# Softmax attention over 128 heads of eight features: a sixth exponential per group on the vector engine, squares on GpSimd, and keys, queries and squares loaded in another order

## The chip, the cores and the metric

The kernel runs on one core of one Trainium2 chip. The engines are called as the profile calls them: PE (TensorE, matmuls), PEld (its weight loads), ACT (ScalarE), DVE (VectorE), POOL (GpSimd) and SP (SyncE, which here only issues DMAs). The metric is the device time of one execution in microseconds (us); lower is better. A median over several executions is given, and one further execution was taken with the hardware profiler.

## The reference, cut to what matters

Four graph layers work on a matrix of 3327 nodes by 128 features, each as `x = x + layer(relu(layernorm(x)), adj)`. The first of them is the one this document is about:

```python
def _L0_gnn_ref(x, spatial_encoding, edge_encoding, Wq, Wk, Wv, Wo):
    n, d = x.shape                      # 3327, 128
    h = Wq.shape[0] // d                # 8
    scale = d ** (-0.5)
    q = (x @ Wq.T).reshape(d, n, h)
    k = (x @ Wk.T).reshape(d, n, h)
    v = (x @ Wv.T).reshape(d, n, h)
    a = jnp.einsum('dnh,dmh->dnm', q, k) * scale
    a = a + spatial_encoding + edge_encoding       # both are adj
    a = jax.nn.softmax(a, axis=2)
    out = jnp.einsum('dnm,dmh->dnh', a, v)
    return out.reshape(n, h * d) @ Wo.T
```

So there are d = 128 independent heads, each with a 3327 x 3327 score matrix of inner length 8, to which twice the adjacency matrix is added before the softmax. The other three layers are two hyperbolic graph layers and a degree-normalised message layer; they multiply the adjacency matrix with a 3327 x 128 matrix and are not touched.

## The kernel before, in words

The program has three stretches. In the first (to about 420 us of the profiled span) the queries, keys and values of all heads are made and written to HBM. The second, the attention, runs from about 420 to 10170 us. The third does the other layers.

**Tiling of the attention.** The scores are made transposed: keys lie on the 128 partitions, queries on the free axis. The 3327 queries are cut into seven chunks `c` of `CW` = 476 columns (the last has 472). The 128 heads form 32 groups `g` of four heads `j`. The 26 tiles of 128 keys form 13 pairs `q` of two tiles (`r` = 0 and 1). The loops run over `c`, then `g`, then `q`; one pair is called `u`, and there are 7 x 32 x 13 = 2912 of them in 224 groups.

**What is done for one pair.** Each of the two key tiles has one PSUM bank of the seven banks of `S`. `seed` (L645, DVE) writes the bank with adjacency minus a bound (`a - shb`, both tiles in SBUF). `scores` (L654, PE) adds the first head's products; `exps` (L666, ACT) reads both banks at once, 952 columns, and writes the exponentials `e`. For head `j` + 1 the matmul adds that head's products and takes away those of head `j` in the same pass: the stacked queries `QS` hold the head's rows and the negated rows of the head before. So a pair's four exponentials follow one another in the same two banks. Where the two banks are not neighbours (one pair in seven) ACT does two instructions of 476 columns instead (L669). `values` (L713, PE) multiplies `e` with the values `VA` and accumulates in one further bank, `po`, over the 13 pairs of a group; after that `store` copies it out on DVE (L721) and sends it off with four DMAs from POOL's queue (L725).

**Exponentials by hand.** In the pairs `q` of `BY_HAND` = (0, 2, 5, 7, 10), the exponential of head 0 on tile r = 1 is not done by ACT but by DVE, with a polynomial (`hand_exp`). There the bank is not seeded for head 0. DVE reads the bare scores out of the bank into the tile `h` (L691), then seeds the bank, then does three scalar_tensor_tensor steps (L695) and a last one (L697) that multiplies by the exponential of adjacency minus bound (`EA`, made once per chunk by `shifted`, L678, and `bare`, L683). Head 1 then uses `QZ`, queries without the negated rows. ACT does one instruction of 476 columns for that slot instead of one of 952.

**The order is written out by hand.** The loop `for i in range(-4, 4 * n + 15)` issues one slot `i` at a time under `tc.manual_schedule()`: the order in which instructions are issued here is the order on each engine. Slot `i` holds the exponential of head `j = -i % 4` of pair `u = (i - 3j) / 4`, so ACT alternates between four pairs. On odd slots PE gets the scores of the next two slots and then eight value matmuls (four heads of one tile; each is two instructions in the profile). DVE gets, in the order of slots that belong to a pair u by hand: at 4u the copy L691 and `seed(u, 1)`, at 4u+1 `seed(u+1, 1)`, at 4u+2 `seed(u+2, 0)`, at 4u+3 the first polynomial step, at 4u+4 two more, at 4u+7 the last. `heads_of` makes the value matmul that needs the hand-made exponential come one pair late.

**Loads.** `loads(u)` is called in the slot 4u and loads the next group: `load_k` (L551, 16 DMAs of 16 partitions), `load_q` (L562 and L564: six small DMAs for a head, nine for head 1), `load_v` (L575). `negate_q` (L570) copies head j's queries negated into the rows of head j + 1, after which `load_q` of head j + 1 overwrites half the rows; so these follow one another: load 0, negate 0, load 1, negate 1, load 2, negate 2, load 3. `spread_v` (L580) and `all_here` (L584, a tiny copy that waits for all key loads) are on POOL. All loads are issued from SP's queue, in the order of the program. For the next chunk, `load_adj` (L590) loads 26 adjacency tiles during the last group, and 22 times in the attention a `Square` of the adjacency matrix is transposed for later use: `load` (L283, with a small memset on POOL, L284), `turn` (L288, DVE), `largest` (L292, DVE) and `store` of 1.66 MB. `plan` puts these in slots.

Of the kernel before, what the change touches and what calls it, by code (L numbers as in the profile page):

```python
# [10 lines left out]
F32 = mybir.dt.float32  # L11
# [6 lines left out]
ALU = mybir.AluOpType  # L18
# [4 lines left out]
P = 128  # L23
N = 3327
D = 128
H = 8
HD = D * H
NT = 26
NP = NT * P
NQ = NT // 2  # L30

KW = NP // 4
HEADS = D
# [3 lines left out]
CW = 476  # L37
# [8 lines left out]
NOTHING = -1.0e30  # L46


EXP_C = (0.9999990463256836, 2.2162604331970215, 2.4563632011413574, 1.8291265964508057)
EXP_ARG = 0.9023826718330383  # L50
BY_HAND = (0, 2, 5, 7, 10)
LN_EPS = 1e-5
L1_EPS = 1e-7
L1_MAX_TANH = 1.0 - 1e-6
# [34 lines left out]
def gnn_kernel(ctx: ExitStack, tc: tile.TileContext, x, adj, Wq, Wk, Wv, Wo, embed, layer,  # L89
               embed_bias, layer_bias, weight, bias, W_in, W_out, out):  # L90
    nc = tc.nc
# [14 lines left out]
    kS_d = dram.tile([2, H, HEADS, NP], F32, name="kS_d")  # L106
# [418 lines left out]
    with tc.tile_pool(name="e1", bufs=1) as e1, tc.tile_pool(name="e_adj", bufs=28) as e_adj, \  # L525
# [12 lines left out]
        S = e_ps.tile([P, 7, 512], F32, name="S")  # L538
        po = e_ps.tile([P, 512], F32, name="po")

        def load_k(c, g):

            b = (c * NG + g) % 2
            for j in range(4):
                d = 4 * g + j
                k0, nk = max(0, j - 1), 1 if j in (0, 3) else 2
                for r in range(2):
                    r0 = 64 * r + 32 * (1 - j % 2)
                    k_d = kS_d[:, :, d, r * NQ * P:(r + 1) * NQ * P].rearrange("i e n -> (i e) n")
                    for i in range(2):  # L550
                        nc.sync.dma_start(KT[b][r0 + 16 * i:r0 + 16 * i + 16, k0:k0 + nk, :].bitcast(F32),  # L551
                                          k_d.unsqueeze(1).to_broadcast([16, nk, NQ * P]))

        def load_q(c, g, j):

# [11 lines left out]
        def negate_q(c, g, j):  # L567

            b, w = (c * NG + g) % 2, width_of(c)
            nc.gpsimd.tensor_scalar(QS[b][:, j + 1, :w], QS[b][:, j, :w].bitcast(F32),  # L570
                                    -1.0, 0.0, op0=ALU.mult, op1=ALU.add)

        def load_v(c, g):
            v = e2.tile([P, 4, NT * H], F32, name="VR", bufs=1)
# [24 lines left out]
        with tc.If(loose < 1), tc.manual_schedule():  # L599
# [39 lines left out]
            def bank(u, r):  # L639
                return S[:, banks(u)[r], :width_of(pairs[u][0])]  # L640
# [19 lines left out]

            def exps(u, j):
                w, (even, odd) = width_of(pairs[u][0]), banks(u)
                e = e_of[u, j] = e_e.tile([P, 2, CW], F32, name=f"e{j}", bufs=(5, 4, 3, 2)[j])
                hand = j == 0 and by_hand(u)
                if even > odd and not hand:
                    touch(u, (0, 1), nc.scalar.activation(e[:, :, :w], S[:, odd:even + 1, :w], AF.Exp, scale=2.0))  # L666
                    return
                for r in range(1 if hand else 2):
                    touch(u, [r], nc.scalar.activation(e[:, 1 - r, :w], bank(u, r), AF.Exp, scale=2.0))  # L669

            def by_hand(u):

                return 0 <= u < n and pairs[u][2] in BY_HAND

            def shifted(c, q):

                w = width_of(c)
                nc.vector.tensor_tensor(EA[q][:, :w], adj_of[c][2 * q + 1][:, :w], shift_of[c][:, :w], op=ALU.subtract)  # L678

            def bare(c, q):  # L680

# [3 lines left out]
            def hand_exp(u):  # L685


                w = width_of(pairs[u][0])
                s = e_h.tile([P, CW], F32, name="h")[:, :w]
                e = e_of[u, 0][:, 0, :w]  # L690
                touch(u, [1], nc.vector.tensor_scalar(s, bank(u, 1), EXP_ARG, None, op0=ALU.mult))  # L691
                seed(u, 1)
                yield
                for k in (3, 2, 1):
                    nc.vector.scalar_tensor_tensor(e, s if k == 3 else e, EXP_C[k], s, op0=ALU.add, op1=ALU.mult)  # L695
                    yield
                nc.vector.scalar_tensor_tensor(e, e, EXP_C[0], EA[pairs[u][2]][:, :w], op0=ALU.add, op1=ALU.mult)  # L697

            def heads_of(u, r):


                first = (u, r)
                if by_hand(u) and r == 1:
                    first = (u + 1, 0)
                elif by_hand(u - 1):
                    first = (u, 1) if r == 0 else (u - 1, 1)
                return [first] + [(u, r)] * 3

            def values(u, r):
                c, g, q = pairs[u]  # L710
                w, k = width_of(c), c * NG + g
                for j, (v, of) in enumerate(heads_of(u, r)):
                    nc.tensor.matmul(po[32 * j:32 * j + H + 1, :w], VA[k % 2][:, 2 * pairs[v][2] + of, j, :],  # L713
                                     e_of[v, j][:, 1 - of, :w], start=(q == 0 and r == 0),
                                     stop=(q == NQ - 1 and r == 1))

            def store(u):
# [9 lines left out]
            def loads(u):  # L727

                c, g, q = pairs[u]
                k = c * NG + g  # L730
                if k + 1 < NC * NG:
                    nxt = divmod(k + 1, NG)
                    if q == 1:
                        load_k(*nxt)
                        load_q(*nxt, 0)
                        v_of[k + 1] = load_v(*nxt)
                    if q in (3, 5, 7):
                        negate_q(*nxt, q // 2 - 1)
                        load_q(*nxt, q // 2)
                    if q == 8:  # L740
                        spread_v(*nxt, v_of.pop(k + 1))
                        here[k + 1] = all_here(*nxt)
                if c + 1 < NC and (g, q) == (0, 0):
                    plan_squares(c)
                if g == NG - 1 and c + 1 < NC:
                    if q == 0:
                        shift_of[c + 1] = load_shift(c + 1)
                        adj_of[c + 1] = []
                    while len(adj_of[c + 1]) < min(NT, 2 * q + 6):
                        adj_of[c + 1].append(load_adj(c + 1, len(adj_of[c + 1])))  # L750


# [2 lines left out]
            def plan(u, f, *a):  # L755
                behind.setdefault(u, []).append((f, a))

            def plan_squares(c):
                for k, s in enumerate(range(squares_of(c), squares_of(c + 1))):
                    sq, u = Square(e_t, s), (c * NG + 7 * k + 1) * NQ  # L760
                    for j in range(4):
                        plan(u, sq.load, j)
                        plan(u + 4, sq.turn, j, 0)
                        plan(u + 9, sq.turn, j, 1)
                        plan(u + 12, sq.largest, j)
                        u += NQ
                    for k, f in ((0, sq.gather), (1, sq.back), (7, sq.finish), (8, sq.store)):
                        plan(u + k, f)

            v0 = load_v(0, 0)  # L770
            load_k(0, 0)
            load_q(0, 0, 0)
            shift_of[0] = load_shift(0)
            for j in range(3):
                negate_q(0, 0, j)
                load_q(0, 0, j + 1)
            spread_v(0, 0, v0)
            here[0] = all_here(0, 0)
            adj_of[0] = [load_adj(0, t) for t in range(NT)]

            for c in range(NC):
                for q in BY_HAND:
# [724 lines left out]
```

## Time and profile before

| what | value |
|---|---|
| median of 3 executions | 10982.34 us (10980.81 to 10985.29) |
| the profiled execution's own time | 10981.96 us |
| its span in the profile | 10980.2 us |
| granted TensorE clock, mean | 0.985 |
| busy: PE, ACT, DVE, POOL | 10533.5, 10033.1, 8487.1, 1529.1 us |
| first and last exponential of the attention (start) | 462.5 and 10167.6 us |
| DMA | 1256.98 MB, mean 114 GB/s |

The attention takes 88 per cent of the span, 9705 us for 224 groups, 43.3 us each. Busy time is the time in which at least one instruction of the engine is open; ACT's and PE's instructions overlap with their followers, so a busy share near 100% does not yet say that the engine could not go faster. In the timeline a row gives the start in us, the length in us, the engine, the line, what is written from what, how many instructions of a kind followed one another, and in brackets the idle time before the row and what ended it.

### The profile page before, as it was taken

To read this page: it belongs to the slowest core of one execution; us is meant where nothing else is said; L and a number is where in the kernel's file an instruction comes from. 1 tells how busy PE (TensorE), PEld (TensorE's weight loads), DVE (VectorE), ACT (ScalarE), POOL (GpSimd) and SP (SyncE) were. 2 spreads that over 40 slices of the span, in tenths; PEclk is the share of its full clock that TensorE was granted. 3 is DMA by queue.
4 is the path that set the end of the run, shared out by engine and by line. 5 is a ranking of instruction groups with operands and counts; after the bars stand their busy time and mean duration, and the time that the engine had idled before them with its cause. 6 is when DMAs were issued, how large, how long until landed. Compare 5 with 4: busy or idle time off the path is not lost. (4 is left out here: it accounts for less than half of the span.)

```text
span 10980.2 us, 204474 instructions
## 1 busy us (share of the span) xinstructions
PE 10533.5 (96%) x72876; PEld 3435.7 (31%) x72876; DVE 8487.1 (77%) x13503; ACT 10033.1 (91%) x13789; POOL 1529.1 (14%) x2477
## 2 busy tenths in 40 slices
PE   4599999999999999999999999999999999999889
PEld 2133333333333333333333333333323333333544
DVE  5588887888878887788887888878877777777655
ACT  3599999999999999999999999999999999999330
POOL 5011111111111111111111111111111111111101
PEclk7799999999999999999999999999999999999999
DMA  8766566565566565565556565565556555554668
GB/s 250 250 99 97 94 96 113 93 98 96 89 118 97 93 97 88 106 98 97 90 95 119 94 96 93 95 119 95 87 93 98 96 95 86 82 88 71 206 233 281
DMA packets 695339, 1256.98 MB, mean 114 GB/s; under 512 B 195218, under 2 KB 555049, under 8 KB 691244
## 3 DMA queue, kind: packets, MB, share of 16 engines
q1 hardware_dynamic: 644044, 1114.42, 55.7%
q0 software_dynamic: 50272, 129.37, 4.3%
q8 instruction: 587, 9.62, 0.4%
q14 instruction: 436, 3.57, 0.2%
HBM read 1096.53 MB, written 146.60 MB: 113 GB/s over the span
## 5 line engine op out<-in xcount | busy, mean ns | idle before, releaser
L666 ACT ACTIVATE e<-S 128x952 f32<-128x952 f32 (+1 forms) x9024 | 8357.9, 1099 | 36.7 <-PE S L654 29.4
L713 PE MATMUL po<-e,VA 128*9 128x476 f32 (+1 forms) x46592 | 5737.5, 564 | 33.0 <-DVE OS L721 12.3
L645 DVE TENSOR_TENSOR S<-a,shb 128x476 f32<-128x476 f32 (+1 forms) x5824 | 3937.9, 676 | 1447.6 <-ACT e L666 1059.4
L654 PE MATMUL S<-QS,KT 64*128 64x476 f32 (+1 forms) x22176 | 4528.6, 445 | 79.7 <-DMA a<-adjT 28.4
L654 PEld LDWEIGHTS S<-QS,KT 64*128 64x128 f32 x22176 | 2073.7, 184 | 5100.5 <-issue 1301.3
L669 ACT ACTIVATE e<-S 128x476 f32<-128x476 f32 (+1 forms) x4128 | 2467.5, 711 | 1.1 <-PE S L654 0.6
L695 DVE SCALAR_TENSOR_TENSOR e<-e,h 128x476 f32<-128x476 f32 (+1 forms) x2240 | 1497.8, 669 | 77.0
L713 PEld LDWEIGHTS po<-e,VA 128*9 128x9 f32 x46592 | 691.0, 88 | 1606.6 <-issue 1488.1
L570 POOL TENSOR_SCALAR QS<-QS 128x476 fp32r<-128x476 f32 (+1 forms) x672 | 485.6, 723 | 4312.1 <-DMA QS<-qS_d 2612.2
L725 POOL DMA_DIRECT2D oT_d<-OS x896 | 470.5, 530 | 3668.8 <-DVE OS L721 3625.5
L691 DVE TENSOR_SCALAR h<-S 128x476 f32<-128x476 f32 (+1 forms) x1120 | 728.0, 650 | 300.9 <-PE S L654 296.5
L697 DVE SCALAR_TENSOR_TENSOR e<-e,EA 128x476 f32<-128x476 f32 (+1 forms) x1120 | 759.6, 678 | 0.0
L695 DVE SCALAR_TENSOR_TENSOR e<-h 128x476 f32<-128x476 f32 (+1 forms) x1120 | 743.1, 663 | 0.0
L1107 PE MATMUL pu<-strip,y 128*128 128x512 f32 (+2 forms) x1456 | 600.5, 566 | 31.7 <-DVE y L968 14.8
L654 PE MATMUL S<-QZ,KT 64*128 64x476 f32 (+1 forms) x1120 | 493.4, 441 | 11.9 <-DVE S L645 10.5
L1107 PEld LDWEIGHTS pu<-strip,y 128*128 128x128 f32 (+1 forms) x1456 | 271.9, 191 | 305.8 <-issue 272.1
L1111 DVE TENSOR_REDUCE deg<-strip 128x1 f32<-128x1536 f32 (+1 forms) x104 | 193.8, 1881 | 63.7 <-DMA strip<-adjT 44.1
L580 POOL COPY VA<-VR 128x832 f32<-128x832 f32 x224 | 242.3, 1082 | 0.0
L654 PEld LDWEIGHTS S<-QZ,KT 64*128 64x128 f32 x1120 | 205.1, 183 | 92.2 <-DVE S L645 52.4
L288 DVE STREAM_TRANSPOSE cols<-rows 128x416 f32<-128x416 f32 x208 | 204.5, 988 | 30.3 <-DMA rows<-in_adj_dram 22.6
L1060 ACT COPY uT<-pu 128x512 f32<-128x512 f32 (+1 forms) x21 | 11.1, 555 | 222.6 <-PE pu L1107 222.6
L721 DVE COPY OS<-po 128x476 f32<-128x476 f32 (+1 forms) x224 | 146.3, 653 | 87.3 <-PE po L713 87.3
(255 smaller groups left out, 1958.6 us busy)
## 6 DMA issues: line engine op xcount, KB each, us to landing
KT<-kS_d SPq DMA_DIRECT2D x1792, 208.0 KB
KT<-kS_d SPq DMA_DIRECT2D x1792, 104.0 KB
VR<-v_d SPq DMA_DIRECT2D x224, 416.0 KB
QS<-qS_d SPq DMA_DIRECT2D x3072, 14.9 KB
QS<-qS_d SPq DMA_DIRECT2D x1536, 29.8 KB
adjT<-cols SPq DMA_DIRECT2D x26, 1664.0 KB
a<-adjT SPq DMA_DIRECT2D x156, 238.0 KB
strip<-adjT POOLq DMA_DIRECT2D x39, 895.5 KB, 5.1
```

What stands on the lines that cost most here:

```text
L570: nc.gpsimd.tensor_scalar(QS[b][:, j + 1, :w], QS[b][:, j, :w].bitcast(F32), -1.0, 0.0, op0=ALU.mult, op1=ALU.add)
L580: nc.gpsimd.tensor_copy(VA[(c * NG + g) % 2][:, :, :, 0:H], v.rearrange("p j (t e) -> p t j e", e=H))
L645: touch(u, [r], nc.vector.tensor_tensor(bank(u, r), adj_of[c][2 * q + r][:, :w], shift_of[c][:, :w], op=ALU.subtract))
L654: x = nc.tensor.matmul(bank(u, r), KT[b][64 * r:64 * r + 64, max(0, j - 1), q * P:(q + 1) * P], q_s[64 * r:64 * r + 64, :w], start=hand an ...
L666: touch(u, (0, 1), nc.scalar.activation(e[:, :, :w], S[:, odd:even + 1, :w], AF.Exp, scale=2.0))
L669: touch(u, [r], nc.scalar.activation(e[:, 1 - r, :w], bank(u, r), AF.Exp, scale=2.0))
L691: touch(u, [1], nc.vector.tensor_scalar(s, bank(u, 1), EXP_ARG, None, op0=ALU.mult))
L695: nc.vector.scalar_tensor_tensor(e, s if k == 3 else e, EXP_C[k], s, op0=ALU.add, op1=ALU.mult)
L697: nc.vector.scalar_tensor_tensor(e, e, EXP_C[0], EA[pairs[u][2]][:, :w], op0=ALU.add, op1=ALU.mult)
L713: nc.tensor.matmul(po[32 * j:32 * j + H + 1, :w], VA[k % 2][:, 2 * pairs[v][2] + of, j, :], e_of[v, j][:, 1 - of, :w], start=(q == 0 and r ...
L725: nc.gpsimd.dma_start(oT_d[:, d * N + c * CW:d * N + c * CW + w], o[32 * j:32 * j + H + 1, :w])
L1107: nc.tensor.matmul(ps[:, :k], y[:m, t, :], s[:m, c * 4 * P - c0:c * 4 * P - c0 + k], start=(t == 0), stop=(t == NT - 1))
```

## The change

* A sixth pair is done by hand: `BY_HAND` becomes (0, 2, 4, 6, 8, 10).
* The polynomial has another form. DVE copies out the scores plus a constant (`z`), POOL squares `z` (a `tensor_tensor` on GpSimd), and DVE does three scalar_tensor_tensor steps. DVE does four instructions per hand exponential where it did five, and POOL one.
* None of DVE's later steps is issued in the slot 4u+3 any more: two are issued at 4u+4 and the last at 4u+7, as far as the next pair is not by hand. `heads_of` is gone; the value matmuls are all in their normal place, and `e0` has four buffers where it had five.
* `negate_q` goes from POOL to DVE. The queries of heads 1, 2 and 3 are loaded in pairs 6, 8 and 10 (3, 5 and 7 before), each right after the negation of the head before. The queries of head 0 are issued ahead of the keys.
* The keys are loaded by 12 DMAs of 32 partitions. The values are loaded in pair 3 (1 before), and `spread_v` and `all_here` go to pair 12 (8 before).
* A square is loaded in pair 3 (0 before), turned in pairs 10 and 12 (4 and 9 before), and stored in pair 2 of the group after (8 before). Adjacency tiles for the next chunk are loaded two tiles later.
* The loads of the very first group are reordered: all queries, the shift and four adjacency tiles, the keys, the values, the other adjacency tiles; its negations are six POOL instructions on 32 partitions each.

```diff
-BY_HAND = (0, 2, 5, 7, 10)
+Q_AT = (1, 6, 8, 10)
+BY_HAND = (0, 2, 4, 6, 8, 10)
...
-        def load_k(c, g):
+        def load_k(c, g, j):
...
+                for k in range(k0, k0 + nk):
+                    nc.sync.dma_start(KT[b][r0:r0 + 32, k, :].bitcast(F32), bass.AP(
...
-            nc.gpsimd.tensor_scalar(QS[b][:, j + 1, :w], QS[b][:, j, :w].bitcast(F32),
-                                    -1.0, 0.0, op0=ALU.mult, op1=ALU.add)
+            nc.vector.tensor_scalar(QS[b][:, j + 1, :w], QS[b][:, j, :w].bitcast(F32), -1.0, None, op0=ALU.mult)
...
-                e = e_of[u, j] = e_e.tile([P, 2, CW], F32, name=f"e{j}", bufs=(5, 4, 3, 2)[j])
+                e = e_of[u, j] = e_e.tile([P, 2, CW], F32, name=f"e{j}", bufs=(4, 4, 3, 2)[j])
...
-                touch(u, [1], nc.vector.tensor_scalar(s, bank(u, 1), EXP_ARG, None, op0=ALU.mult))
+                touch(u, [1], nc.vector.tensor_scalar(z, bank(u, 1), EXP_C[0], None, op0=add))
+                nc.gpsimd.tensor_tensor(e, z, z, op=mult)
                 seed(u, 1)
                 yield
-                for k in (3, 2, 1):
-                    nc.vector.scalar_tensor_tensor(e, s if k == 3 else e, EXP_C[k], s, op0=ALU.add, op1=ALU.mult)
-                    yield
-                nc.vector.scalar_tensor_tensor(e, e, EXP_C[0], EA[pairs[u][2]][:, :w], op0=ALU.add, op1=ALU.mult)
-
-            def heads_of(u, r):
...
+                v(z, e, EXP_C[1], z, op0=add, op1=add)
+                yield
+                v(e, e, EXP_C[2], z, op0=add, op1=mult)
+                yield
+                v(e, e, EXP_C[3], EA[pairs[u][2]][:, :w], op0=add, op1=mult)
...
+                    if q in Q_AT:
+                        j = Q_AT.index(q)
+                        if j:
+                            negate_q(*nxt, j - 1)
+                        load_q(*nxt, j)
                     if q == 1:
-                        load_k(*nxt)
-                        load_q(*nxt, 0)
+                        for j in range(4):
+                            load_k(*nxt, j)
+                    if q == 3:
                         v_of[k + 1] = load_v(*nxt)
-                    if q in (3, 5, 7):
-                        negate_q(*nxt, q // 2 - 1)
-                        load_q(*nxt, q // 2)
-                    if q == 8:
+                    if q == 12:
                         spread_v(*nxt, v_of.pop(k + 1))
                         here[k + 1] = all_here(*nxt)
...
-                        plan(u, sq.load, j)
-                        plan(u + 4, sq.turn, j, 0)
-                        plan(u + 9, sq.turn, j, 1)
+                        plan(u + 3, sq.load, j)
+                        plan(u + 10, sq.turn, j, 0)
+                        plan(u + 12, sq.turn, j, 1)
...
-                    for k, f in ((0, sq.gather), (1, sq.back), (7, sq.finish), (8, sq.store)):
+                    for k, f in ((0, sq.gather), (1, sq.back), (2, sq.store), (7, sq.finish)):
...
+            for j in range(4):
+                load_q(0, 0, j)
+            shift_of[0] = load_shift(0)
+            adj_of[0] = [load_adj(0, t) for t in range(4)]
+            for j in range(4):
+                load_k(0, 0, j)
             v0 = load_v(0, 0)
...
-                for k in range(0 if at % 3 else 1 if at else 0 if by_hand(i // 4) else 2):
+                for k in range(0 if at % 3 or by_hand(i // 4) else 1 if at else 2):
```

More of the change, by code (lines that the diff above doesn't have):

```diff
@@ L46 @@
 NOTHING = -1.0e30
-EXP_C = (0.9999990463256836, 2.2162604331970215, 2.4563632011413574, 1.8291265964508057)
-EXP_ARG = 0.9023826718330383
-BY_HAND = (0, 2, 5, 7, 10)
+EXP_C = (0.25674915313720703, 0.05050157010555267, 1.8002841472625732, 0.8117094039916992)
+EXP_LEAD = -0.2054332047700882
+Q_AT = (1, 6, 8, 10)
+BY_HAND = (0, 2, 4, 6, 8, 10)
 LN_EPS = 1e-5
@@ L539, in gnn_kernel @@
         po = e_ps.tile([P, 512], F32, name="po")
-        def load_k(c, g):
+        def load_k(c, g, j):
             b = (c * NG + g) % 2
[L544 to L552, printed above, removed]
+            d = 4 * g + j
+            k0, nk = max(0, j - 1), 1 if j in (0, 3) else 2
+            for r in range(2):
+                r0 = 64 * r + 32 * (1 - j % 2)
+                for k in range(k0, k0 + nk):
+                    nc.sync.dma_start(KT[b][r0:r0 + 32, k, :].bitcast(F32), bass.AP(
+                        tensor=kS_d.tensor, offset=kS_d.offset + d * NP + r * NQ * P,
+                        ap=[[0, 2], [H * HEADS * NP, 2], [HEADS * NP, 8], [1, NQ * P]]))
         def load_q(c, g, j):
@@ L677, in shifted @@
                 w = width_of(c)
-                nc.vector.tensor_tensor(EA[q][:, :w], adj_of[c][2 * q + 1][:, :w], shift_of[c][:, :w], op=ALU.subtract)
+                nc.vector.scalar_tensor_tensor(EA[q][:, :w], adj_of[c][2 * q + 1][:, :w], EXP_LEAD, shift_of[c][:, :w],
+                                               op0=ALU.add, op1=ALU.subtract)
             def bare(c, q):
@@ L688, in hand_exp @@
                 w = width_of(pairs[u][0])
-                s = e_h.tile([P, CW], F32, name="h")[:, :w]
+                v, add, mult = nc.vector.scalar_tensor_tensor, ALU.add, ALU.mult
+                z = e_h.tile([P, CW], F32, name="h")[:, :w]
                 e = e_of[u, 0][:, 0, :w]
-                touch(u, [1], nc.vector.tensor_scalar(s, bank(u, 1), EXP_ARG, None, op0=ALU.mult))
+                touch(u, [1], nc.vector.tensor_scalar(z, bank(u, 1), EXP_C[0], None, op0=add))
+                nc.gpsimd.tensor_tensor(e, z, z, op=mult)
                 seed(u, 1)
                 yield
-                for k in (3, 2, 1):
-                    nc.vector.scalar_tensor_tensor(e, s if k == 3 else e, EXP_C[k], s, op0=ALU.add, op1=ALU.mult)
-                    yield
-                nc.vector.scalar_tensor_tensor(e, e, EXP_C[0], EA[pairs[u][2]][:, :w], op0=ALU.add, op1=ALU.mult)
-            def heads_of(u, r):
[L702 to L707, printed above, removed]
+                v(z, e, EXP_C[1], z, op0=add, op1=add)
[3 more added lines that the diff above has]
+                v(e, e, EXP_C[3], EA[pairs[u][2]][:, :w], op0=add, op1=mult)
             def values(u, r):
@@ L711, in values @@
                 w, k = width_of(c), c * NG + g
-                for j, (v, of) in enumerate(heads_of(u, r)):
-                    nc.tensor.matmul(po[32 * j:32 * j + H + 1, :w], VA[k % 2][:, 2 * pairs[v][2] + of, j, :],
-                                     e_of[v, j][:, 1 - of, :w], start=(q == 0 and r == 0),
+                for j in range(4):
+                    nc.tensor.matmul(po[32 * j:32 * j + H + 1, :w], VA[k % 2][:, 2 * q + r, j, :],
+                                     e_of[u, j][:, 1 - r, :w], start=(q == 0 and r == 0),
                                      stop=(q == NQ - 1 and r == 1))
@@ L748, in loads @@
                         adj_of[c + 1] = []
-                    while len(adj_of[c + 1]) < min(NT, 2 * q + 6):
+                    while len(adj_of[c + 1]) < min(NT, 2 * q + 4):
                         adj_of[c + 1].append(load_adj(c + 1, len(adj_of[c + 1])))
@@ L761, in plan_squares @@
                     for j in range(4):
-                        plan(u, sq.load, j)
-                        plan(u + 4, sq.turn, j, 0)
-                        plan(u + 9, sq.turn, j, 1)
+                        plan(u + 3, sq.load, j)
+                        plan(u + 10, sq.turn, j, 0)
+                        plan(u + 12, sq.turn, j, 1)
                         plan(u + 12, sq.largest, j)
                         u += NQ
-                    for k, f in ((0, sq.gather), (1, sq.back), (7, sq.finish), (8, sq.store)):
+                    for k, f in ((0, sq.gather), (1, sq.back), (2, sq.store), (7, sq.finish)):
                         plan(u + k, f)
+            for j in range(4):
+                load_q(0, 0, j)
+            shift_of[0] = load_shift(0)
+            adj_of[0] = [load_adj(0, t) for t in range(4)]
+            for j in range(4):
+                load_k(0, 0, j)
             v0 = load_v(0, 0)
-            load_k(0, 0)
-            load_q(0, 0, 0)
-            shift_of[0] = load_shift(0)
+            adj_of[0] += [load_adj(0, t) for t in range(4, NT)]
             for j in range(3):
-                negate_q(0, 0, j)
-                load_q(0, 0, j + 1)
+                for r0 in (32 * (1 - j % 2), 64 + 32 * (1 - j % 2)):
+                    nc.gpsimd.tensor_scalar(QS[0][r0:r0 + 32, j + 1, :CW], QS[0][r0:r0 + 32, j, :CW].bitcast(F32),
+                                            -1.0, 0.0, op0=ALU.mult, op1=ALU.add)
             spread_v(0, 0, v0)
             here[0] = all_here(0, 0)
-            adj_of[0] = [load_adj(0, t) for t in range(NT)]
             for c in range(NC):
```

## The prediction

> **What bounds the kernel now.** I read the page's busy line and its groups first, then the timeline of one group in the middle of the attention.
>
> ```profile
> PE 10533.5 (96%) x72876; PEld 3435.7 (31%) x72876; DVE 8487.1 (77%) x13503; ACT 10033.1 (91%) x13789; POOL 1529.1 (14%) x2477
> L666 ACT ACTIVATE e<-S 128x952 f32<-128x952 f32 (+1 forms) x9024 | 8357.9, 1099 | 36.7 <-PE S L654 29.4
> L645 DVE TENSOR_TENSOR S<-a,shb 128x476 f32<-128x476 f32 (+1 forms) x5824 | 3937.9, 676 | 1447.6 <-ACT e L666 1059.4
> L669 ACT ACTIVATE e<-S 128x476 f32<-128x476 f32 (+1 forms) x4128 | 2467.5, 711 | 1.1 <-PE S L654 0.6
> ```
>
> PE and ACT both look full. The timeline tells them apart, by the distance of starts and not by lengths:
>
> ```profile
> 5003.73 0.99 PE L713 MATMUL po<-e,VA 128*9 128x476 f32 x8
> 5003.94 0.65 ACT L669 ACTIVATE e<-S 128x476 f32<-128x476 f32 x1
> 5004.38 6.20 ACT L666 ACTIVATE e<-S 128x952 f32<-128x952 f32 x7
> 5005.29 0.99 PE L713 MATMUL po<-e,VA 128*9 128x476 f32 x8
> 5006.83 0.99 PE L713 MATMUL po<-e,VA 128*9 128x476 f32 x8
> 5010.30 1.21 ACT L669 ACTIVATE e<-S 128x476 f32<-128x476 f32 x2
> ```
>
> Seven wide exponentials take 5010.30 - 5004.38 = 5.92 us, 0.846 each; a narrow one takes 5004.38 - 5003.94 = 0.44. At these prices all exponentials take 9024 x 0.846 + 4128 x 0.445 = 9470 us of the 9705 us between the first and the last (462.5 to 10167.6): ACT is the bound, with 235 us lost, 1.05 per group. PE needs 1.54 us for two slots (5005.29 to 5006.83) where ACT needs 1.69, but only 1.29 where one of the two is by hand. Over two pairs with one hand exponential ACT takes 7 x 0.846 + 0.445 = 6.37 (6.41 with the narrow pairs) and PE 4 x 1.54 = 6.16. PE is thus close behind, and a late seed soon becomes lost ACT time.
>
> **What ACT saves.** Per group one slot goes from 0.846 to 0.445, or in one pair of seven from 0.89 to 0.445: 0.407 on the mean, x 224 = 91 us. One more `bare` per chunk gives back 3. Gain 88.
>
> **What DVE and POOL get.** DVE: 6 x 4 hand steps instead of 5 x 5, plus three negations; about +1.3 us per group of 43.3 at 0.65 each, at 77% busy: no bound by its sum. POOL: six squares. Line L369, the same operation, gives the price by two sizes:
>
> ```profile
> L369 POOL TENSOR_TENSOR sq<-sq 128x512 f32<-128x512 f32 x52 | 65.9, 1268 | 28.5 <-ACT sq L367 27.4
> L369 POOL TENSOR_TENSOR sq<-sq 128x256 f32<-128x256 f32 x52 | 37.6, 722 | 4.2
> L226 DVE TENSOR_SCALAR h<-h 128x3328 f32<-128x3328 f32 x1 | 1.9, 1850 | 0.0
> L225 DVE TENSOR_TENSOR h<-h,s 128x3328 f32<-128x3328 f32 x1 | 3.6, 3624 | 0.0
> ```
>
> (1268 - 722) / 256 = 2.13 ns a column: 1.19 us for 476. By its time alone a square is hidden: it starts after L691 in slot 4u, and the step that needs it comes in slot 4u+4. What it does to DVE beside it is the question. The timeline has the like already, where POOL's copy of VA falls next to a hand exponential:
>
> ```profile
> 1233.45 0.65 DVE L691 TENSOR_SCALAR h<-S 128x476 f32<-128x476 f32 x1 [0.38 <-PE S L654]
> 1234.14 0.66 DVE L645 TENSOR_TENSOR S<-a,shb 128x476 f32<-128x476 f32 x1
> 1235.19 0.88 POOL L580 COPY VA<-VR 128x832 f32<-128x832 f32 x1
> 1235.51 1.84 DVE L645 TENSOR_TENSOR S<-a,shb 128x476 f32<-128x476 f32 x2 [0.70 <-ACT e L666]
> 1236.05 2.08 ACT L666 ACTIVATE e<-S 128x952 f32<-128x952 f32 x2
> 1236.19 1.15 PE L654 MATMUL S<-QS,KT 64*128 64x476 f32 x4
> 1238.02 1.02 ACT L669 ACTIVATE e<-S 128x476 f32<-128x476 f32 x2
> ```
>
> The two seeds begin at 1235.51 and take 1.84 us; elsewhere the same two take 1.43 (5015.48). The first ends only 0.5 us after the copy has ended (1236.07), so it did nothing until then. The scores that wait for it take 1.15 instead of 0.70, and ACT's two slots 1.97 (1236.05 to 1238.02) instead of 1.69: 0.28 us lost. Steps with one SBUF input, such as L691 from PSUM, keep their 0.65 beside POOL. In the other direction VA copies that begin while a seed runs are 1.30 long: POOL waits for that one seed, then goes first. The Trainium skill, "SBUF — State Buffer", section "Who interferes with whom", says why: a DVE instruction with two SBUF inputs and a GpSimd instruction that reads SBUF share a port pair, which one of them holds to its end. By that rule every square holds up DVE; without it (and without the row) the sum would be the 88 us gain and the start's 10.
>
> **The path through a hand pair.** Time 0 is the start of L691. It ends at 0.65; `seed(u, 1)` runs 0.69 to 1.35 (rows 1233.45, 1234.14). POOL wants to square at about 0.9, waits for that seed, and then holds until 1.35 + 1.19 - 0.14 = 2.40 (the 0.14 is start-up, done during the wait: 1.30 - 0.56 of waiting = 0.74, against 0.88 alone). `seed(u+1, 1)`, in row 1235.51 free to go at 2.06, ends at 2.40 + 0.5 = 2.90, and its scores start at 2.95. Without a square they start between 2.6 and 2.75 (1236.19 - 1233.45 = 2.74, late as shown). From there PE needs two rounds (3.08) to the scores of pair u+2, 0.55 more to the next L691 (scores 5002.93, L691 5003.48 in the timeline), and again 2.95: 6.58 for two pairs where ACT needs 6.41. That is 0.17 us lost for each hand pair that follows another at distance two and has no negation: 2 and 4.
>
> In pairs 6, 8 and 10 `negate_q` stands between the two seeds on DVE. Row L226 does 3328 columns from SBUF to SBUF in half the time of L225, so a negation takes about 0.45. Bounds: free, if it runs beside the square as L691 would; or it too stands until 2.40, and `seed(u+1, 1)` ends 0.32 later. I take the second, since at the doubled rate it moves two elements at a time through DVE's SBUF side, as the two-input steps do. So 0.49 for each of these three.
>
> The same section of the skill also says that a DVE instruction in a mode that uses both ports contends with GpSimd; no row here shows one beside POOL, and by that page it is the second bound.
>
> Pair 0 follows pair 10 at distance three: 4 x 1.54 + 0.55 + 2.95 = 9.66, and ACT needs 9.8: nothing.
>
> Sum: 224 x (2 x 0.17 + 3 x 0.49) = 405 us. Of the 235 us that ACT loses already, the largest item stays: when `po` is copied out (L721) PE waits, "PEld po <- DVE OS" 118.5 us in the waits, and ACT loses some 68 us at the first slot of pair 4, by the distances of its starts. The other 167 are waits for the same chain and are replaced. Net cost 238.
>
> **Moved steps at nothing, and what covers them.** Leaving out `heads_of`: the last step still comes in slot 4u+7, the value matmul in 4u+13, 5 us later. Four `e0` buffers: the matmuls of pair u stand on PE ahead of the scores of pair u+4. Turns of squares in pairs 10 and 12 (0.99 us each): the first lies beside the square, the second where no hand step follows. `spread_v` and `all_here`, right behind the square of pair 10: the copy stood there before as well (9.9 pairs into the group).
>
> The negations make DVE wait for query loads, with all seeds behind them. Before, POOL's negations followed each other by 4.2 to 4.4 us (4992.83, 4997.03, 5001.35), that is SP's issues and the landing; now two pairs, 6.6 us, lie between. Cover 2.2 us. If it goes, in the 22 groups where a square's store of 1.66 MB and the values are queued ahead of query load 1, a wait could be up to 5 us, 110 in all. Key loads hold SP for 13.56 us (4968.80, 16 issues) from the start of a group and the last query before lands near pair 7; 12 issues, with only head 0's queries ahead, don't land later. I take 0.
>
> **The first group.** SP starts at 419.75, the first score at 461.18. Now: 27 query issues x 0.35 = 9.5, shift and four tiles 2.7, keys 12/16 of 16.77 = 12.6, landing and values 4.5, VA copy and `seen` 1.1: 450. Between 0 and 15 us saved; I take 10.
>
> **Sum.** 10981.96 - 88 + 238 - 10 = 11122 us, from the profiled execution, which is 0.4 us under the median. For the doubt over the landing of the queries I add a quarter of the 110 us, hence 11150.
>
> **Rivals.** (1) Slack takes up the holds: PE's rounds absorb each, and the gain appears whole, 10982 - 98 = 10884. For it: DVE idles 1447 us before seeds, waiting for ACT, so a square in that gap costs nothing. It decides if the held seed ends by 2.75 after L691 instead of 2.90, which is a square of 1.04 us or less. Against it: L369's two rows. (2) Squares hold, negations don't: 224 x 5 x 0.17 = 190 - 167 - 98 = -75, 10907, or 10990 if half of the old losses stay. Against it: L226's rate. (3) On top of my forecast DVE waits for queries, 11122 + 110 and the same again in smaller pieces over the other groups (224 x 0.2 = 45): 11277. Against it: 2.2 us of cover.
>
> **How the numbers follow.** Forecast 0.54, rival 1 0.13, rival 2 0.20, rival 3 0.13. The forecast's own range is 11040 to 11230 (the 167 us kept or not; a negation's hold 0.2 to 0.4). The range 10930 to 11270 leaves out rival 1, a third of rival 2 and half of rival 3. About 0.2% can be told from no change. Faster: rival 1, half of rival 2, a little of the forecast, 0.26; same 0.06; slower 0.68.
>
> **What would show it.** Right: the group S<-a,shb at 720 ns or more instead of 676; POOL's squares near 1.3 to 1.7 us; seeds behind a hand pair lengthened to a GpSimd end; ACT's idle before L666 grown, named PE S; 43.9 to 44.2 us per group. The narrow exponentials rise by 160 in count (192 wide ones become narrow, 32 narrow ones go). Wrong: seeds still at 676, groups of 42.9 us. Rival 3 shows as waits of QS on DVE for DMA, of several us.

## The result, and the profile after

The changed kernel takes 18061.14 us (median of 4, 18059.74 to 18071.63) against 10983.82 before: a ratio of 1.6445, 95% interval 1.6424 to 1.6466. The prediction, 11150, had the direction and missed nearly all of the size. Of the 7077 us, about 6660 are one thing that the prediction had costed at nothing, the new form of the key loads. With the old form the change costs 3.9%, nearly all of it waits that can be avoided; the same kernel without them is 0.9% faster than the one before.

Of before, the page's DMA row (busy share in 40 slices of the span, in tenths) and the row of a group's key loads on SP:

```profile
DMA  8766566565566565565556565565556555554668
...
4968.80 13.56 SPq L551 DMA_DIRECT2D KT<-kS_d  x16
```

The page after, the lines that answer to those shown of before, and DMA's:

```profile
PE 11110.7 (62%) x72876; PEld 3571.2 (20%) x72876; DVE 8854.5 (49%) x13955; ACT 10047.2 (56%) x13764; POOL 2915.2 (16%) x3155
...
DMA  8211112111121111121111211112111111111157
...
q1 hardware_dynamic: 592076, 1114.22, 19.6%
...
L665 ACT ACTIVATE e<-S 128x952 f32<-128x952 f32 (+1 forms) x8832 | 8200.1, 1060 | 5807.0 <-PE S L653 5783.2
...
L644 DVE TENSOR_TENSOR S<-a,shb 128x476 f32<-128x476 f32 (+1 forms) x5824 | 4102.3, 704 | 1353.6 <-ACT e L665 1006.2
...
L693 POOL TENSOR_TENSOR e<-h 128x476 f32<-128x476 f32 (+1 forms) x1344 | 1847.4, 1375 | 13678.8 <-DVE h L692 12646.7
L570 DVE TENSOR_SCALAR QS<-QS 128x476 fp32r<-128x476 f32 (+1 forms) x669 | 543.5, 812 | 6403.4 <-DMA QS<-qS_d 6278.8
```

No engine is the bound any more: ACT's share is 56% where it was 91%, its work nearly the same (10047 us against 10033). Two lines belong together: ACT idles 5783 us for scores, and DVE idles 6279 us ahead of the negation L570, for query loads. The DMA row looks idle, one to two tenths, where it was five to six tenths with the same 1114 MB on SP's queue: this kernel waits for DMA while DMA is hardly busy, which points to a transfer that is confined, not to one that is large. The timeline of one group shows it, SP's rows first, then DVE's and ACT's:

```profile
9018.08 27.85 SPq L550 DMA_DIRECT2D KT<-kS_d  x12
9046.05 8.72 SPq L284 DMA_DIRECT2D rows<-in_adj_dram  x4
...
9063.84 0.31 SPq L562 DMA_DIRECT2D QS<-qS_d  x1
```

```profile
9040.01 1.18 DVE L570 TENSOR_SCALAR QS<-QS 128x476 fp32r<-128x476 f32 x1
...
9075.76 0.41 DVE L570 TENSOR_SCALAR QS<-QS 128x476 fp32r<-128x476 f32 x1 [28.95 <-DMA QS<-qS_d]
```

```profile
9077.59 0.96 ACT L665 ACTIVATE e<-S 128x952 f32<-128x952 f32 x1 [28.61 <-PE S L653]
```

Twelve key issues hold SP for 27.85 us (16 took 13.56 before), and the query load that is due in pair 6 leaves at 9063.84. The negation of pair 8 waits 28.95 us for it, every seed stands behind the negation on DVE, and ACT waits 28.61. Each group has this once: 73.7 us at the median, 43.2 before (the group shown also loads a part of a square, the row at 9046.05; the last chunk, which has no squares, has 71.7). How the keys move is seen in the windows (start and end, length, then busy time of PE, PEld, DVE, ACT and POOL, granted clock, DMA share, GB/s), before and after:

```profile
4968.00:4984.00 16.00, 15.72 (x112) 4.88 (x112) 12.40 (x20) 15.85 (x22) 2.10 (x4) 1.00 0.87 126
```

```profile
9018.00:9046.00 28.00, 27.86 (x212) 8.58 (x204) 24.25 (x37) 28.00 (x41) 7.52 (x9) 1.00 0.14 52
9046.00:9070.00 24.00, 2.67 (x21) 0.78 (x13) 0.77 (x2) 2.98 (x5) 1.38 (x1) 0.63 0.27 82
```

A DMA share of 0.14 is 2.2 engines of 16. In the trace's packet records the 384 key packets of a group (6656 bytes each) take 0.27 us on the mean with 2.0 open at a time, 51 us in all; before, 0.74 us with 14.1 open, some 20 us (medians over the 224 groups). Each packet is faster alone, but only two run, though twelve DMAs stand in the queue. The new source begins with a dimension of two copies, `[0, 2]`. The Trainium skill, "DMA: Bandwidth & Descriptors", section "Rules for kernel authors", has the rule: an outermost dimension of c below 16, for instance a leading broadcast of c copies, leaves the DMA at most c engines. The trace agrees with c = 2, and an experiment below with 8. The rule spoke against the change, and I had read only the number of issues.

### The profile page after: what moved, and what is told of

Same layout as the page of the kernel before. It is cut to its first block, busy times and chain, and to the rows that moved or that the text cites. A ratio compares the mean times of both kernels' runs of the same rounds, so it can differ in the third digit from the quotient of the medians.

```text
span 18058.3 us, 206056 instructions
## 1 busy us (share of the span) xinstructions
PE 11110.7 (62%) x72876; PEld 3571.2 (20%) x72876; DVE 8854.5 (49%) x13955; ACT 10047.2 (56%) x13764; POOL 2915.2 (16%) x3155
## 4 chain that ended last, share of the span: by engine, by line
PE 43%; DMA 37%; SPq 8%; DVE 5%; issue 3%; ACT 2%; POOL 0%; DVEq 0%; POOLq 0%; ACTq 0%
PE po L706 22%; DMA KT<-kS_d 20%; PE S L653 17%; DMA rows<-in_adj_dram 9%; DMA QS<-qS_d 6%; SPq L550 3%; PE pu L1107 3%; SPq L574 2%; DVE S L644 2%; DMA a<-adjT 1%; ACT e L665 1%; DVE h L692 1%; DVE OS L714 1%; SPq L284 1%; SPq L296 0%
## 5 line engine op out<-in xcount | busy, mean ns | idle before, releaser
L665 ACT ACTIVATE e<-S 128x952 f32<-128x952 f32 (+1 forms) x8832 | 8200.1, 1060 | 5807.0 <-PE S L653 5783.2
L653 PE MATMUL S<-QS,KT 64*128 64x476 f32 (+1 forms) x21952 | 4794.2, 463 | 6394.9 <-DVE S L644 6330.1
L706 PE MATMUL po<-e,VA 128*9 128x476 f32 (+1 forms) x46592 | 6025.9, 591 | 27.9
L644 DVE TENSOR_TENSOR S<-a,shb 128x476 f32<-128x476 f32 (+1 forms) x5824 | 4102.3, 704 | 1353.6 <-ACT e L665 1006.2
L693 POOL TENSOR_TENSOR e<-h 128x476 f32<-128x476 f32 (+1 forms) x1344 | 1847.4, 1375 | 13678.8 <-DVE h L692 12646.7
L570 DVE TENSOR_SCALAR QS<-QS 128x476 fp32r<-128x476 f32 (+1 forms) x669 | 543.5, 812 | 6403.4 <-DMA QS<-qS_d 6278.8
L692 DVE TENSOR_SCALAR h<-S 128x476 f32<-128x476 f32 (+1 forms) x1344 | 874.0, 650 | 599.7 <-PE S L653 581.3
L698 DVE SCALAR_TENSOR_TENSOR e<-e,h 128x476 f32<-128x476 f32 (+1 forms) x1344 | 878.5, 654 | 46.0
L696 DVE SCALAR_TENSOR_TENSOR h<-e,h 128x476 f32<-128x476 f32 (+1 forms) x1344 | 869.6, 647 | 0.0
L653 PE MATMUL S<-QZ,KT 64*128 64x476 f32 (+1 forms) x1344 | 609.9, 454 | 202.2 <-DVE S L644 202.2
L289 DVE STREAM_TRANSPOSE cols<-rows 128x416 f32<-128x416 f32 x208 | 204.5, 988 | 22.0 <-DMA rows<-in_adj_dram 13.9
```

The costliest lines, as they stand in the source:

```text
L570: nc.vector.tensor_scalar(QS[b][:, j + 1, :w], QS[b][:, j, :w].bitcast(F32), -1.0, None, op0=ALU.mult)
L644: touch(u, [r], nc.vector.tensor_tensor(bank(u, r), adj_of[c][2 * q + r][:, :w], shift_of[c][:, :w], op=ALU.subtract))
L653: x = nc.tensor.matmul(bank(u, r), KT[b][64 * r:64 * r + 64, max(0, j - 1), q * P:(q + 1) * P], q_s[64 * r:64 * r + 64, :w], start=hand an ...
L692: touch(u, [1], nc.vector.tensor_scalar(z, bank(u, 1), EXP_C[0], None, op0=add))
L693: nc.gpsimd.tensor_tensor(e, z, z, op=mult)
L696: v(z, e, EXP_C[1], z, op0=add, op1=add)
```

## The experiments

**The old key loads in the changed kernel**, all else as changed.

```diff
-                for k in range(k0, k0 + nk):
-                    nc.sync.dma_start(KT[b][r0:r0 + 32, k, :].bitcast(F32), bass.AP(... ap=[[0, 2], [.., 2], [.., 8], [1, NQ * P]]))
+                for i in range(2):
+                    nc.sync.dma_start(KT[b][r0 + 16 * i:r0 + 16 * i + 16, k0:k0 + nk, :].bitcast(F32),
+                                      k_d.unsqueeze(1).to_broadcast([16, nk, NQ * P]))
```

> The changed kernel with the key loads alone as they were before (16 DMAs of 16 partitions per group, the partitions being the outermost dimension of the source); order of loads, six hand exponentials, squares on GpSimd and negations on DVE stay. Theory A (each new key DMA has an outermost dimension of 2 and is served by two DMA engines at a time, so a group's keys take 51 us instead of 20): nearly all of the loss goes, groups of 43 to 44.5 us, 10880 to 11250 us in all; what is left over 10984 is the price of the holds between GpSimd and DVE. Theory B (the order does it: queries late in the group, with DVE waiting for them): groups stay over 50 us, more than 12500 us. Theory C (the holds of squares cost far more than the 0.17 to 0.49 us estimated): no DMA waits, but 45 us or more per group, over 11400 us.

Measured: 11401.51 us, ratio 1.0387 (1.037 to 1.0404). 6660 us are gone. What is left: normal groups of 43.7 us (43.2 before), some 105 us in all; 22 groups of about 56 us, 12.5 more each, 275 us; six last groups of a chunk at 51.0 against 44.7, 37 us. That is 150 us over the first theory's range, which took what is left to be the price of the holds alone: two thirds of it stand in the 22 groups, and the waits name them (total us, times, the longest; some are of other groups):

```profile
DVE QS L570 <- DMA QS<-qS_d: 285.1, 48, 12.5
```

**The new key loads in the kernel before**, nothing else.

> The kernel before with the new key DMAs alone (12 of 32 partitions, outermost dimension 2). Theory A: the keys of a group take about 51 us, the four query loads follow one another behind them for some 14 us, so groups of 60 to 68 us, 14700 to 16500 us. Theory B and C: the key DMAs alone cost nothing, 10950 to 11050 us.

Measured: 16751.31, ratio 1.5258 (1.5228 to 1.5289), packets again 2.0 at a time, 51 us a group. The first theory's mechanism holds, its upper end was 250 us too low. The form of the loads is enough by itself, 5770 us; with the negation still on POOL, that engine waits 11444.9 us for queries.

**Key loads with eight as outermost dimension**: 48 DMAs of eight partitions in the changed kernel.

```diff
+                    for i in range(4):
+                        nc.sync.dma_start(KT[b][r0 + 8 * i:r0 + 8 * i + 8, k, :].bitcast(F32),
+                                          kS_d[i % 2, :, d, r * NQ * P:(r + 1) * NQ * P])
```

> The changed kernel with the key loads cut into 48 DMAs of 8 partitions (outermost dimension 8). Theory A: eight DMA engines carry one DMA, the packets of 6656 bytes take 0.25 to 0.5 us each, 384 x 0.25 to 0.5 / 8 = 12 to 24 us per group, which is hidden: within 1% of the run with 16 partitions. If instead the number of partitions on the SBUF side counts and not the outermost dimension, 8 partitions are slower than 32: keys of more than 51 us and over 18000 us.

Measured: 11983.57, ratio 1.0916. Packets of 0.44 us, 7.2 at a time, 24 us a group (21 to 30). The width follows the outermost dimension, 2, 8 and 16 giving 2.0, 7.2 and 14.1, and neither the number of issues (12, 48, 16) nor that of partitions in one DMA (32, 8, 16) puts the three in this order. An outermost dimension of two that is no repeated copy was not run. But 24 us were not hidden as I expected: the kernel is 5% slower than with 16, and L570 waits 737 us, since query load 1 stands behind the keys. (This run also has four times the issues of the changed kernel, so the 5% is not the transfer's alone.)

The next four start from the first of these kernels (11401 us) and take its three remaining waits one at a time.

**The square's store in pair 11.**

```diff
-                    for k, f in ((0, sq.gather), (1, sq.back), (2, sq.store), (7, sq.finish)):
+                    for k, f in ((0, sq.gather), (1, sq.back), (7, sq.finish), (11, sq.store)):
```

> The after kernel with the old 16 key loads, and the square's store issued in pair 11 of the group instead of pair 2. Theory A (the 22 long groups are long because the store of 1.66 MB and the values are queued ahead of query loads 1 and 2, so that the negation on DVE waits some 12.5 us for a landing, with all seeds behind it): the 22 groups fall from about 56 to 44 us, 22 x 12.5 = 275 us less than the 11401 of the kernel with 16 key loads, 11110 to 11160. Rival B (the long groups come from what the square itself takes from DVE and PE: its two turns, its load): 11380 or more, and the waits of QS on DVE for DMA stay. If the store merely shifts the wait to the next group's first loads (keys behind it in the queue), about half of the gain, 11200 to 11300.

Measured: 11308.1, 93 us less, a third of the 275: groups of 49 to 53 where 44 was expected. The store was one part; the other was found later.

**VA's copy on DVE.**

```diff
-            nc.gpsimd.tensor_copy(VA[(c * NG + g) % 2][:, :, :, 0:H], ...)
+            nc.vector.tensor_copy(VA[(c * NG + g) % 2][:, :, :, 0:H], ...)
```

> The after kernel with the old 16 key loads, and spread_v's copy of VA done by DVE instead of POOL. Theory A (POOL's copy, issued directly behind the square of pair 10, takes the port pair over from it, so that seed(u+1, 1) of pair 10 ends 3.75 us after L692 instead of 3.0, and ACT loses 0.875 us at the first slot of pair 11): the stall at that slot falls to about 0.25, as at pairs 7 and 9, 0.6 x 224 = 135 us less than 11401, 11230 to 11290, the copy's own time on DVE being hidden (it comes in pair 12, which has no hand step). Rival B (the negation and the store of squares make that stall, or DVE's copy of 832 columns delays the seeds just as much): 11380 or more.

Measured: 11268.97, 133 us less, as expected. ACT's stall at the first slot of pair 11 fell from 0.875 us to 0.30; a normal group takes 43.1.

**Negations where no square is under way.**

```diff
-Q_AT = (1, 6, 8, 10)
+Q_AT = (1, 7, 9, 11)
```

> The after kernel with the old 16 key loads, and the negations and the query loads behind them in pairs 7, 9 and 11 instead of 6, 8 and 10, where no square is under way. Theory A (the negation reads and writes SBUF in a mode that cannot run beside POOL's square; it stands for 0.8 us and then delays seed(u+1, 1) by 0.31): negations take 0.36 us each instead of 1.18; the stalls of 0.22 and 0.26 us at the first slots of pairs 7 and 9 go; pair 11's stays at 0.5 to 0.875 because VA's copy is there still. About 0.5 to 0.8 us a group, 110 to 180 us less than 11401: 11220 to 11300. Rival B (the chain behind a square is late by itself, as I sized it at 0.17 us a pair, and the negation adds nothing): within 20 us of 11401. In the groups with a square's store the wait for queries should stay about 12 us under both.

Measured: 11194.68, 207 us less, more than expected: normal groups of 42.58 us (median), 1.17 less, while the 22 long ones grew from 56.0 to 57.6. The stalls at pairs 7 and 9 are gone, and that at pair 11 fell too, from 0.875 to 0.11, with VA's copy still on POOL. The negations took 0.40 us each. The timeline of pair 10 says why, DVE then POOL, first with the negation in pair 10:

```profile
4987.74 1.01 DVE L289 STREAM_TRANSPOSE cols<-rows 128x416 f32<-128x416 f32 x1
4988.66 0.38 DVE L570 TENSOR_SCALAR QS<-QS 128x476 fp32r<-128x476 f32 x1
4988.94 2.12 DVE L644 TENSOR_TENSOR S<-a,shb 128x476 f32<-128x476 f32 x2
```

```profile
4987.28 1.39 POOL L693 TENSOR_TENSOR e<-h 128x476 f32<-128x476 f32 x1 [5.32 <-DVE h L692]
4988.61 1.17 POOL L579 COPY VA<-VR 128x832 f32<-128x832 f32 x1
```

and with the negation in pair 11:

```profile
4898.35 0.99 DVE L289 STREAM_TRANSPOSE cols<-rows 128x416 f32<-128x416 f32 x1
4899.27 1.87 DVE L644 TENSOR_TENSOR S<-a,shb 128x476 f32<-128x476 f32 x2
```

```profile
4897.88 1.38 POOL L693 TENSOR_TENSOR e<-h 128x476 f32<-128x476 f32 x1 [5.26 <-DVE h L692]
4899.21 1.41 POOL L579 COPY VA<-VR 128x832 f32<-128x832 f32 x1
```

In the first, the copy begins at the square's end, the negation has just been served, and the seeds at 4988.94 take 2.12 us for two: the copy holds them until 4989.78. In the second the seed stands ready when the square ends and goes first; it is the copy that is longer (1.41). In both groups DVE also turns a square here (L289); over all 224 groups `seed(u+1, 1)` of pair 10 ends 3.70 us after the start of L692 at the median with the negation in pair 10, and 2.69 with it in pair 11. So a chain of three, square, negation, copy, made that stall, and either edit breaks it. That the two engines take turns at the port is read from these two timelines and not tested by itself.

**All three together.**

> All three edits together on the after kernel with the old 16 key loads: the store in pair 11, VA's copy on DVE, the negations in pairs 7, 9 and 11. Theory A (the three waits are separate): 11401 - 275 - 135 to 195 - 60 to 110 = 10820 to 10930, faster than the kernel before by 0.4 to 1.4%; groups of about 42.6 us. Rival B (PE's two rounds per pair or ACT's own time are next in line and take back half): 10950 to 11050.

Measured: 11078.54, ratio 1.0087 (1.0071 to 1.0104). That is above both ranges. Normal groups are as expected, 42.6, but the 22 are still 50.5 to 55. SP's rows in one of them (its group begins at 673.4):

```profile
672.35 1.75 SPq L300 DMA_DIRECT2D rowmax_d<-rm  x4
680.77 0.38 SPq L305 DMA_DIRECT2D four<-rowmax_d  x1
681.25 1.35 SPq L562 DMA_DIRECT2D QS<-qS_d  x1
...
684.46 13.36 SPq L551 DMA_DIRECT2D KT<-kS_d  x16
```

Between L300 and L305 SP stands for 6.7 us: L305 (`back`) reads what L300 (`gather`) writes. In these 22 groups query 0, with the keys behind it, leaves 7.5 us after the group's first exponential, in the others 2.9 us before it (medians).

**The read-back later**, on top of the three.

```diff
-((0, sq.gather), (1, sq.back), (7, sq.finish), (11, sq.store))
+((0, sq.gather), (8, sq.back), (11, sq.store), (12, sq.finish))
```

> The kernel with all three edits (11079), and the read-back of a square's row maxima (L305) moved from pair 1 to pair 8 of the group after the square, its last step to pair 12. Theory A (in the 22 groups of 51 to 54 us SP stands for 6 to 8 us before L305, whose DMA waits for the one that writes the maxima, so that query 0 and the 16 key loads are issued 8 us late, query load 1 lands behind them, and the negation waits about 9 us on DVE): the 22 groups fall to about 43.5, 22 x 8.5 = 187 us less, 10880 to 10910, faster than the kernel before by 0.7 to 1%. Rival B (it is the store of 1.66 MB that holds the queries back, wherever L305 stands): less than 60 us gained, 11020 to 11070.

Measured: 10886.34, ratio 0.9913 (0.9896 to 0.9929), the fastest kernel of this study. 192 us are 8.7 for each of the 22 groups, which now take 42.4 to 43.4; query 0 leaves 0.8 us after their first exponential. The edit also moves the square's last step, whose DMA stood ahead of query load 1 on SP; what each of the two moves gave was not parted. L305 stood in pair 1 in the kernel before too, where POOL waited for the queries and no seed stood behind it.

```profile
L665 ACT ACTIVATE e<-S 128x952 f32<-128x952 f32 (+1 forms) x8832 | 8311.7, 1133 | 41.3 <-PE S L653 38.0
...
L570 DVE TENSOR_SCALAR QS<-QS 128x476 fp32r<-128x476 f32 (+1 forms) x669 | 268.5, 401 | 35.2 <-DMA QS<-qS_d 30.7
```

**More cover for the negations**: queries in pairs 1, 3, 7 and 11, and the store in pair 12.

> On top of that, the query loads of heads 0 to 3 in pairs 1, 3, 7 and 11 (so that each negation comes four pairs, 13 us, after the load that it waits for, where 6.6 us lay between), and the store of the square in pair 12, behind the last query load. Theory A (what remains are negations that wait for queries in the six groups in which the next chunk's adjacency is loaded, 46 to 50 us each, and in groups with a square): 20 to 40 us less than the run before it, 10850 to 10880. Rival B (what remains there is not the negations but EA waiting for the adjacency tiles themselves, 3.2 us before L677): within 10 us of it.

Measured: 11290.13, 404 us slower: both theories failed. The two edits were then parted, with the store back in pair 11.

> The kernel with the query loads in pairs 1, 3, 7 and 11, with the store of the square back in pair 11 (as in the 10886 run), so that only the pairs of the query loads differ from that run. Theory A (the 11290 us came from the store in pair 12: it stands directly ahead of query 0 and the keys of the next group, in the queues, and ahead of L311 on SP): the long groups go, 10860 to 10920. Rival B (it came from the pairs of the queries: query load 1 is now issued with the key loads still in the queues, and only lands behind them, so that the negation in pair 7 waits 6 to 7 us in the groups with a square): 11100 to 11290.

Measured: 11111.57 (two runs), in the rival's range. So 225 us came from the pairs of the queries and 179 from the store one pair later. In the 11290 run the negation of pair 7 of one such group waits 6.73 us; query load 1 was issued just before (703 to 712 us in the timeline), as it now comes behind the 16 key issues, which end at 701.5 there. Program distance is not cover if the queue between is full.

**Five by hand instead of six**, on the 11290 kernel.

```diff
-BY_HAND = (0, 2, 4, 6, 8, 10)
+BY_HAND = (0, 2, 4, 6, 10)
```

> The kernel with the loads mended (queries in 1, 3, 7, 11), with five exponentials by hand per group, the one in pair 8 left out. Theory A (with the waits gone ACT is the bound, so a sixth exponential by hand is worth its ACT time of 0.407 us a group, 91 us, less about 0.07 us a group that its chain costs at the pair after): 75 to 91 us slower than with six, 10930 to 10970. Rival B (PE or the seeds are the bound by now, the sixth brings nothing): within 25 us of six.

Measured: 11339.81, 50 us slower than six, between the two theories. The groups with waits hide part of it; in the last chunk, where no square comes between, a group takes 42.70 with five and 42.29 with six, by the distance of the `po` copies: 0.40 us, as the prediction priced a sixth.

**Squares by DVE**, on the 11290 kernel.

```diff
-                nc.gpsimd.tensor_tensor(e, z, z, op=mult)
+                nc.vector.tensor_tensor(e, z, z, op=mult)
```

> The same with six, and the squares done by DVE instead of POOL (0.65 us each, right behind L692). Theory A (POOL's square holds the port for as long as DVE's own square takes: L692, square, seed, seed end at 4 x 0.68 = 2.7 us, the same 2.7 as beside a POOL square; DVE has 6 x 0.65 = 3.9 us more per group and room for it): within 0.3% of the kernel with POOL squares. Rival B (DVE's room between the seeds is what the hand pairs need, and POOL's squares are the gain of this form): slower by 0.5 to 2%.

Measured: 11744.91, 4% slower, twice the rival's upper end; a group of the last chunk takes 44.93 instead of 42.29. `seed(u+1, 1)` does end at 2.68 us, as theory A had it. But the square now stands ahead of `seed(u, 1)`, which ends at 1.92 instead of 1.35, and head 1's scores wait for that bank. The rows of 1250 us of the last chunk, with DVE's squares and with POOL's:

```profile
L653 PE MATMUL S<-QZ,KT 64*128 64x472 f32 x167 | 79.8, 478 | 42.6 <-DVE S L644 39.9
```

```profile
L653 PE MATMUL S<-QZ,KT 64*128 64x472 f32 x178 | 80.4, 452 | 0.0
```

42.6 us over 167/6 groups is 1.53 a group, more than half of the 2.64 by which a group grew. The rest was not taken apart, and a DVE square behind the seed was not tried.

## Why the prediction was wrong, by its steps

**The step that failed** is the sentence on the key loads: "12 issues, with only head 0's queries ahead, don't land later. I take 0." It counted issues, and these are indeed fewer, for the same bytes. It did not ask how many packets of such a DMA run at a time: 2.0 where 14.1 ran before, so that a group's keys took 51 us instead of 20, and 6660 of the 7077 us went with them. (The first group's term has the same fault, "keys 12/16 of 16.77": in the changed kernel the first exponential starts at 491.3 us, 29 us later than before and not 10 earlier.) The mechanism of rival 3, DVE waiting for query loads, then carried the whole cost: 6279 us in the waits against the 155 that I gave it, because I sized it by a square's store and not by the keys. The forecast priced no case with slower keys, so the range could not hold it.

**The rest can be judged on the kernel with the old key loads (11401)**, for which the sum without the doubt over queries was 11122:

| term | predicted | measured |
|---|---|---|
| a sixth by hand, ACT's time | 0.407 us a group | 0.40 (last chunk, five against six) |
| lost ACT time in a normal group, all causes | 1.81 + 0.30 | 1.83 (0.95 before) |
| of it at the first slot of pair 4, where `po` is copied out | stays, 0.30 | 0.00 (0.32 before) |
| a pair without negation (2, 4) | 0.17 each | at most 0.015, at the first slots of pairs 3 and 5 |
| a pair with negation (6, 8) | 0.49 each | 0.22 and 0.26, at those of pairs 7 and 9 |
| pair 10 | 0.49, copy behind it 0 | 0.875 |
| a square's end after the start of L692 | 2.40 | 2.18 |
| `seed(u+1, 1)` ends, without and with negation | 2.90, 3.22 | 2.70, 3.01 |
| query waits in 22 groups | a quarter of 110 | 275 |
| first group | -10 | about 0 |

The hold was right in kind and 0.2 us too long in size. The square takes 0.83 us after the wait, not 1.05, and that moves pairs 2 and 4 under the 2.75 from which rival 1 was said to decide: for these two pairs it was right. The held negation was right: 0.40 us alone (0.45 predicted), 1.18 beside a square. The timeline of pair 6, DVE and POOL:

```profile
5017.59 0.66 DVE L644 TENSOR_TENSOR S<-a,shb 128x476 f32<-128x476 f32 x1
5018.16 1.19 DVE L570 TENSOR_SCALAR QS<-QS 128x476 fp32r<-128x476 f32 x1
```

```profile
5017.70 1.38 POOL L693 TENSOR_TENSOR e<-h 128x476 f32<-128x476 f32 x1 [5.08 <-DVE h L692]
```

The negation ends 0.27 us after the square (5019.08), though alone it needs 0.40 in all. This is the last case that the prediction cited from the Trainium skill, "SBUF — State Buffer", section "Who interferes with whom": a DVE instruction in a mode that uses both ports contends with GpSimd, and the one that comes second is blocked for the whole of the other. The prediction showed no row of it; these agree.

`spread_v` "stood there before as well" was wrong as an argument: the place was the same, the neighbour was not, and behind a square and a negation it cost 0.6 us a group. And the query wait in the 22 groups had two causes, the store (93/22 = 4.2 us), which I had seen, and `back` with the last step that was moved along (8.7), which I had not. In the normal group the errors cancelled, which is luck: predicted +0.67 us, measured +0.55 (43.75 against 43.20, medians). The hand pairs cost less than the sum had at pairs 2 to 8 and more at pair 10, and the loss at pair 4, which was to stay, went; why it went was not tried. A total that fits is not yet a breakdown that fits.

With the old key loads the first exponential moved from 462.5 to 456.3 us, but the first group became 7 us longer (53.6 against 46.7), so nothing of the 10 us came.

**The signs.** POOL's squares at 1.375 us and 160 more narrow exponentials (4288) came as said. Seeds were to be at 720 ns or more and are at 704, the smaller hold. ACT's idle time did grow and is named PE S, but that sign did not part the cases: behind it stood DVE's wait for a DMA. The sign of rival 3, waits of QS on DVE for DMA, is the one that told the truth.

## What to carry to other kernels

When a DMA is rewritten, look first at the outermost dimension of its access pattern and only then at issues and bytes; in this profile, the mark of a confined transfer was a low DMA share with an engine waiting on DMA. When a step that waits for a load moves to another engine, price it by what is queued behind it there, and take its cover from the queue's rows in the worst group, not from program distance. Here two instructions at a shared port cost little (0.22 and 0.26 us); a third right behind them made it 0.875, and moving the negations by a pair (207 us) was worth more than giving the third to another engine (133 us).

## What the runs showed of the hardware that was not expected

The granted clock fell with the idle time: in the 24 us in which PE was busy 2.67 it was 0.63 (0.50 from 9056 on), while the 28 us ahead of it had 1.00. The mean is 0.802 (0.985 before), and PE's busy time grew by 577 us with the same 72876 matmuls.

By the timelines shown, the port between DVE and POOL changes hands at the end of an instruction, and an instruction that waits for it is booked as running: 0.40 us of negation show as 1.18 in its row, and a square of 1.38 has run only 0.83 since the seed ahead of it ended. A long mean in the groups can thus be a wait that no wait view names.
